# Moving the readout product, two sums and the z projection inside a selective-scan stage

## The chip, the cores and the metric

The kernel runs on one core of one Trainium2 chip. The metric is the device time of that core in microseconds. In the text, PE is TensorE (matmuls), DVE is VectorE, ACT is ScalarE, POOL is GpSimd, and SP is the queue from which most DMAs are issued. Each engine runs its own instructions in order.

## The reference

A convolutional attention layer, then a Mamba block in two directions with a small MLP, then a mixture of two chosen experts. The change lies in the Mamba block alone. Cut to what matters, for each direction:

```
xz = x @ in_proj_w.T                  # 256 -> 1024
xc, z = split(xz)                     # 512 channels each
xc = silu(conv4(xc) + conv_b)         # four taps along the tokens
dt, Bm, Cm = split(xc @ x_proj_w.T)   # 16 + 16 + 16
dt = softplus(dt @ dt_proj_w.T + dt_proj_b)
dA = exp(dt * A);  dBx = dt * Bm * xc # 512 channels x 16 states
h_t = dA_t * h_(t-1) + dBx_t;  y_t = sum over states of h_t * C_t
y = (y + xc * Dp) * silu(z);  out = y @ out_proj_w.T
```

The two directions' outputs are added to m. Then come a layer norm, the MLP `leaky_relu(h @ w1.T + b1) @ w2.T + b2`, the addition of m and of the residual x1, and a second layer norm. There are 4096 tokens, all in float32.

## The kernel before, in words

Four phases follow one another: convolution, attention, Mamba, experts. The Mamba phase (`mamba_phase`, from line 1258) is where everything below happens.

The tokens are cut into 8 chunks of 512. A round is one chunk in one direction, so there are 16 rounds, called i (or q while it is being prepared); even rounds go forward, odd ones backward. A round has 32 slots. A slot n is one (i, e, k, j): one of four channel tiles e, one of four groups of states k, one half j of the tile's channel quarters. Its work is a tile of 128 partitions x 1024. Slot 0 of a round is e = 0, k = 0, j = 0; e changes every 8 slots, k every 2.

The work of a slot:
- `inflow` (POOL, L1894): dbx = dt*x times B, issued two slots ahead, into three buffers.
- `decay` (ACT, L1884): da = exp(dt*A), two instructions into one of two PSUM buffers, one slot ahead.
- `recur` (DVE): the scan over 1024 elements (L1907), and right after it the product with C into one of four h buffers (L1912).
- In slots whose place in the round stands in POOLED, the scan writes h itself, and GpSimd makes the product one slot later (`pooled`, L1917).
- `keep` (ACT, L1938): one slot later, the last state is copied out. The next decay follows it on ACT.
- `bring` (ACT L1932, or POOL L1930 in four slots of a round): adds to dbx what the state brings into the second half of the tile.
- `sum_states` (PE, L1945 and L1947): every second slot, the two h tiles are summed over the states into y, in PSUM, where there is one buffer. A pair whose first slot is pooled is summed one slot later.
- `close` (DVE, L1956): after the last states of a tile, y times z into xc's place. It is in the first slot of the next tile, after that slot's product.

Beside the slots, generators are stepped once per slot:
- `prepare(q)` makes the next round's inputs. It starts at slot 27 of the round before last and goes on through the previous round's slots 0 to 29: projection of x (two PSUM buffers `mm`), four conv sums in slots 3 to 7, SiLU in slot 8, x_proj in slot 9, dt_proj in slots 11 to 15, then softplus. Softplus is max(x,0) + log(1 + exp(-|x|)), with a correction rd that keeps the rounding of 1 + exp: `Identity` of -exp - 1 and then + 1 on ACT (L1425, L1426), three identity matmuls that sum rd, exp and the positive part (L1432, slots 18 to 21), a copy back (L1428), and the logarithm in slot 23 (L1436). GpSimd then adds the logarithm to dt (`dt_piece` with v = 0, L1460) and makes dt*x (v = 1, L1471). Both are written to DRAM, from which `load_dt` reads them back spread over the partitions. The first column of dt goes to DRAM too (`first`, L1465); the carried states are made of it.
- z is projected two tiles at a time in slots 23 and 25 (L1437, L1450) and copied by ACT in slots 24 to 27 (L1448).
- `output(i)` projects the closed round in slots 1 to 3 of the next and adds it to m: by ACT (forward) or DVE (backward, L1536).
- `tail(c)` makes the norms and the MLP of a chunk. It has one PSUM buffer `tl`. Each of its steps names the engine it needs next, and it isn't stepped in slots that FULL lists for that engine. GpSimd adds x1 to m (L1552).

Three functions of ACT need a table load each time they alternate with the decay's exponential: SiLU of z in slot 0 (L2023), SiLU of xc in slot 8 (L1391), and the logarithm in slot 23 (L1436).

The order on each engine is written out by hand. It is the order of these calls, and no scheduler moves anything:

```
inflow(n + 2); keep(n - 1); decay(n + 1); bring(n + 1); recur(n)
load_bc / load_dt; pooled(n - 1); sum_states(n - 3 or n - 2); close
step(out); silu of z; step(prep); step(coming); dt_piece; step(tail)
```

Of the kernel before, what the change touches and what calls it, by code (L numbers as in the profile page):

```python
# [14 lines left out]
FP = mybir.dt.float32  # L15
# [9 lines left out]
P = 128  # L25
# [4 lines left out]
N = 512  # L30
# [1227 lines left out]
def mamba_phase(cx, early, w_in, w_x, w_out, w1, w2, x1d, ud, bcd, dtd, x2d, u2d, usum):  # L1258
# [12 lines left out]
    with ExitStack() as ctx:  # L1271
# [51 lines left out]
        for d in range(2):  # L1323
            for e in range(ET):
                nc.vector.tensor_scalar(
                    skip[d][:, e, :].rearrange("q (j p) -> q j p", j=4), cx.ident.rearrange("q (p j) -> q j p", j=4),
                    cx.col(f"dp{d}", e), None, ALU.mult,
                )
        b1c = one.tile([P, FT], FP, name="b1c")
# [29 lines left out]
        def prepare(q):  # L1359
# [35 lines left out]
            for e in range(ET):  # L1395
                nc.tensor.matmul(ps[0:nx, :], wx[d][:, e, :], xc[:, e, :], start=e == 0, stop=e == ET - 1)
            yield
            xd = few()[0:nx, :]
            nc.scalar.copy(xd, ps[0:nx, :])

# [7 lines left out]
            for e in range(ET + 1):  # L1408
                if e > 0:
                    ex = early.wide("ex")[:, :, 0:N] if e == 1 else ex  # L1410
                    dt = dt or sp.tile([P, ET, N], FP, name="dt", tag="dt")
                    nc.scalar.activation(ex[:, e - 1, :], ps, AF.Abs, bias=cx.col(f"dtb{d}", e - 1))
                    nc.scalar.activation(dt[:, e - 1, :], ps, AF.Relu, bias=cx.col(f"dtb{d}", e - 1))
                if e < ET:
                    ps = mm_psum()
                    nc.tensor.matmul(ps, wdt[r, P * e : P * e + P], xd[r, :], start=True, stop=True)
                yield
# [4 lines left out]
            for e in range(ET + 2):  # L1422
                if e < ET:
                    rd = rds[e] = few()
                    nc.scalar.activation(rd, ex[:, e, :], AF.Identity, scale=-1.0, bias=-1.0)  # L1425
                    nc.scalar.add(rd, rd, 1.0)  # L1426
                if e > 1:
                    nc.scalar.copy(dt[:, e - 2, :], sums.pop(e - 2))  # L1428
                if 0 < e <= ET:
                    ps = sums[e - 1] = mm_psum()  # L1430
                    for v, x in enumerate((rds.pop(e - 1), ex[:, e - 1, :], dt[:, e - 1, :])):
                        nc.tensor.matmul(ps, cx.ident, x, start=v == 0, stop=v == 2)  # L1432
                yield
# [3 lines left out]
            zs = in_pair(q, ET)  # L1437
            yield
            got["dt"] = dt
            for at, (v, e) in enumerate(((0, 0), (1, 0), (0, 1), (0, 2), (0, 3), (1, 1))):  # L1440
                if at == 3 and q > 1:
                    load_first(q, 0)
                dt_piece(q, v, e, ex)
                if at in (0, 2):
                    z = sp.tile([P, 2, N], FP, name="z", tag="z", bufs=3)
                    got.setdefault("z", []).append(z)
                if at < 4:
                    nc.scalar.copy(z[:, at % 2, :], zs[at % 2])  # L1448
                if at == 1:
                    zs = in_pair(q, ET + 2)  # L1450
                    if q + 1 < 2 * NCH:
                        load_u(q + 1)
                yield

        def dt_piece(q, v, e, ex=None, eng=nc.gpsimd):
# [3 lines left out]
            if v == 0:  # L1459
                eng.tensor_tensor(dt[:, e, :], dt[:, e, :], ex[:, e, :], ALU.add)  # L1460
                if q < 2:
                    return
                if e == 0:
                    firsts[q] = ip.tile([P, ET], FP, name="first", tag="first", bufs=1)
                nc.gpsimd.tensor_tensor(firsts[q][:, e : e + 1], dt[:, e, 0:1], odd[:, 0:1], ALU.add)  # L1465
                if e % 2:
                    first_rows[q, e // 2] = cx.rows.tile([P, 2], FP, name="first_row", tag="first_row", bufs=2)
                    nc.sync.dma_start(out=first_rows[q, e // 2], in_=firsts[q][:, e - 1 : e + 1])
# [70 lines left out]
        def tail(c):  # L1539
# [3 lines left out]
            yield from layer_norm(cx, tl, tl_psum, m, hn, nc.gpsimd, 2)  # L1543
            x1 = tl.tile([P, CT, N], FP, name="x1", tag="ln_xc")
            nc.sync.dma_start(out=x1, in_=x1d[c])
            for t in range(CT):
# [3 lines left out]
            yield "DMA"  # L1550
            yield "POOL"
            nc.gpsimd.tensor_tensor(m, x1, m, ALU.add)  # L1552
# [320 lines left out]
        firsts, first_rows, got_first, brought = {}, {}, {}, {}  # L1873
# [26 lines left out]
        def recur(n):  # L1900
# [9 lines left out]
            )  # L1910
            if n % SPS not in POOLED:
                nc.vector.tensor_tensor(h, da, bcs[i, k][1][:, None, :].to_broadcast([P, 2, N]), ALU.mult)  # L1912
# [41 lines left out]
        def close(i, e):  # L1954
# [7 lines left out]
        POOLED = {4, 10, 12, 18, 28}  # L1962
# [7 lines left out]
            "PE": {0, 1, 2, 3, 4, 5, 6, 7, 9, 18, 19, 20, 21, 23, 24, 25, 27, 29},  # L1970
            "ACT": {0, 6, 7, 8, 9, 16, 17, 18, 19, 20, 21, 22, 23, 30, 31},
            "POOL": {0, 1, 2, 4, 24, 25, 26, 27, 28, 29, 30, 31},
# [4 lines left out]
        with tc.manual_schedule(engines=ORDERED):  # L1977
# [5 lines left out]
            for n, (i, e, k, j) in enumerate(slots):  # L1983
# [24 lines left out]
                if j == 0 and n > 0:  # L2008
                    if (n - 2) % SPS not in POOLED:
                        sum_states(n - 2)  # L2010
                    if k == 0:
                        close(*slots[n - 2][:2])
                        if e == 0:
                            out = output(i - 1)
# [24 lines left out]
                if tails and (i == 2 * NCH - 1 or at not in FULL[needs[0]]):  # L2039
                    needs[0] = next(tails[0], None)  # L2040
                    if needs[0] is None:
                        tails.pop(0)
                        needs[0] = "PE"
            ending()
# [307 lines left out]
```

## Time and profile before

| what | us |
|---|---|
| median of 3 runs | 4116.2 (4112.8 to 4122.62) |
| the profiled execution | 4114.68 |
| its span, first to last instruction | 4112.9 |
| first and last scan start | 1940.2 and 3801.4 |
| DVE busy in the span | 3499.8 (85%) |
| PE busy in the span | 3584.9 (87%) |
| ACT busy in the span | 2666.2 (65%) |
| POOL busy in the span | 1839.2 (45%) |

The scans run over 1861 us, with 512 slots in them. The shares over the whole span mix phases with different limits, so the busy times of the scan stage alone count here. In a group's line the numbers are: how many instructions, their busy time together, the mean nanoseconds of one, the engine's idle time just before them, and what ended it. A float32 matmul appears as two records in PE's groups. In a timeline a row is start, duration, engine, line, operation, output and inputs, form, count, and in brackets the idle time before it with what ended that.

### The profile page before, as it was taken

To read this page: it belongs to the slowest core of one execution; us is meant where nothing else is said; L and a number is where in the kernel's file an instruction comes from. 1 tells how busy PE (TensorE), PEld (TensorE's weight loads), DVE (VectorE), ACT (ScalarE), POOL (GpSimd) and SP (SyncE) were. 2 spreads that over 40 slices of the span, in tenths; PEclk is the share of its full clock that TensorE was granted. 3 is DMA by queue.
4 is the path that set the end of the run, shared out by engine and by line. 5 is a ranking of instruction groups with operands and counts; after the bars stand their busy time and mean duration, and the time that the engine had idled before them with its cause. 6 is when DMAs were issued, how large, how long until landed. Compare 5 with 4: busy or idle time off the path is not lost. (4 is left out here: it accounts for less than half of the span.)

```text
span 4112.9 us, 43197 instructions
## 1 busy us (share of the span) xinstructions
PE 3584.9 (87%) x14772; PEld 1175.0 (29%) x14772; DVE 3499.8 (85%) x2908; ACT 2666.2 (65%) x4146; POOL 1839.2 (45%) x1283
## 2 busy tenths in 40 slices
PE   6769888999999999997888888888888888876898
PEld 2324332222222222222222222222222222222343
DVE  8998877989888888877899999999999999999211
ACT  1111226988887888875777778778787778775222
POOL 3020000000000000002888889888888989987000
PEclk9889998999999999998888988998989899988899
DMA  6222215223322322214333344343433334432221
GB/s 208 93 98 96 81 58 157 52 60 65 66 62 55 65 63 57 58 39 138 116 103 121 114 137 139 101 141 106 135 106 127 121 124 120 132 118 80 75 68 35
DMA packets 164051, 399.92 MB, mean 97 GB/s; under 512 B 36981, under 2 KB 45941, under 8 KB 163566
## 3 DMA queue, kind: packets, MB, share of 16 engines
q1 hardware_dynamic: 139198, 312.65, 24.0%
q0 software_dynamic: 24624, 84.43, 8.8%
q8 instruction: 118, 1.93, 0.2%
q14 instruction: 111, 0.91, 0.1%
HBM read 268.16 MB, written 79.56 MB: 85 GB/s over the span
## 5 line engine op out<-in xcount | busy, mean ns | idle before, releaser
L1894 POOL TENSOR_TENSOR dbx<-dtxr,b 128x1024 f32<-128x1024 f32 x512 | 1203.7, 2362 | 197.3 <-DMA dtxr<-dtd 91.3
L1046 ACT ACTIVATE e<-sc 128x1024 f32<-128x1024 f32 x1024 | 993.7, 1023 | 172.0 <-PE sc L1039 147.1
L1907 DVE TENSOR_TENSOR_SCAN da<-da,state,dbx 128x1024 f32<-128x1024 f32 x432 | 1013.9, 2347 | 14.6 <-ACT da L1884 7.2
L956 DVE TENSOR_TENSOR s<-s,e 128x1024 f32<-128x1024 f32 x768 | 880.4, 1216 | 25.0 <-ACT e L1046 24.3
L1884 ACT ACTIVATE da<-dtr,aneg 128x512 f32<-128x512 f32 x1024 | 708.0, 691 | 32.6 <-DMA dtr<-dtd 3.1
L1039 PE MATMUL sc<-q,kS 32*128 32x512 f32 x4096 | 651.9, 648 | 18.6 <-ACT e L1046 13.9
L1912 DVE TENSOR_TENSOR h<-da,c 128x1024 f32<-128x1024 f32 x432 | 529.1, 1225 | 33.1 <-PE y L1947 1.3
L963 PE MATMUL av<-e,vT 128*32 128x512 f32 x4096 | 553.6, 611 | 0.0
L979 POOL DMA_DIRECT2D s<-s x94 | 81.6, 879 | 946.5 <-DVE s L956 856.1
L1947 PE MATMUL y<-h,sel 128*32 128x512 f32 x2048 | 376.1, 664 | 91.6 <-DVE h L1912 66.4
L464 PE MATMUL cv<-v,u 128*128 128x512 f32 x928 | 414.6, 607 | 28.8 <-DVE v L288 13.3
L1039 PEld LDWEIGHTS sc<-q,kS 32*128 32x128 f32 x4096 | 211.4, 185 | 460.7 <-issue 253.1
L1341 PE MATMUL mm<-u,win 128*128 128x512 f32 x464 | 253.6, 697 | 77.6 <-ACT z L1448 25.8
L464 PEld LDWEIGHTS cv<-v,u 128*128 128x128 f32 x928 | 179.4, 195 | 261.7 <-issue 227.8
L562 DVE SCALAR_TENSOR_TENSOR acc<-pad,wdw_s,acc 128x768 f32<-128x768 f32 (+1 forms) x192 | 236.0, 1234 | 19.9 <-ACT acc L555 14.2
L1938 ACT COPY state<-da 128x2 f32<-128x2 f32 x431 | 67.9, 158 | 265.6 <-DVE h L1912 264.7
L143 POOL TENSOR_TENSOR ln_few<-ln_few,minus_half 128x4 f32<-128x4 f32 x29 | 37.4, 1291 | 400.5 <-DMA ln_few<-ln_row 265.4
L1387 PE MATMUL mm<-xp,taps 128*128 128x512 f32 x480 | 213.0, 596 | 0.1
L956 DVE TENSOR_TENSOR s<-e 128x1024 f32<-128x1024 f32 x128 | 151.9, 1217 | 59.5 <-ACT e L1046 59.3
L1907 DVE TENSOR_TENSOR_SCAN h<-da,state,dbx 128x1024 f32<-128x1024 f32 x80 | 187.5, 2344 | 10.6 <-ACT state L1938 9.9
L963 PEld LDWEIGHTS av<-e,vT 128*32 128x32 f32 x4096 | 81.4, 108 | 397.0 <-issue 389.2
L1917 POOL TENSOR_TENSOR h<-h,c 128x1024 f32<-128x1024 f32 x80 | 188.6, 2357 | 1.0 <-ACT state L1938 1.0
(382 smaller groups left out, 3922.1 us busy)
## 6 DMA issues: line engine op xcount, KB each, us to landing
dtr<-dtd SPq DMA_DIRECT2D x128, 512.0 KB
dtxr<-dtd SPq DMA_DIRECT2D x128, 512.0 KB
s<-s POOLq DMA_DIRECT2D x94, 512.0 KB, 6.0
b<-bcd SPq DMA_DIRECT2D x64, 256.0 KB
c<-bcd SPq DMA_DIRECT2D x64, 256.0 KB
dtd<-dt SPq DMA_DIRECT2D x64, 256.0 KB
dtd<-few SPq DMA_DIRECT2D x64, 256.0 KB
u<-uv SPq DMA_DIRECT2D x24, 640.0 KB
```

Source lines behind the costliest of these rows:

```text
L464: nc.tensor.matmul(rows4(ps), u[:, dy, P * ci : P * ci + P], v[:, dy : dy + HR, ci, :], start=dy + ci == 0, stop=dy == k - 1 and ci == CT - 1,
L562: nc.vector.scalar_tensor_tensor(o, src, w_ap, o, ALU.mult, ALU.add)
L956: nc.vector.tensor_tensor(z, x, y, ALU.add)
L963: nc.tensor.matmul(g.av[32 * h : 32 * h + 32, :], vT[:, kb, P * t + 32 * h : P * t + 32 * h + 32], es[h // 2][:, h % 2, :], start=kb == 0, ...
L1039: nc.tensor.matmul(ps[h // 2][:, h % 2, :], kS[r, t, P * kb : P * kb + P], q_t[r, t, :], start=True, stop=True,)
L1046: nc.scalar.activation(e, ps[i], AF.Exp)
L1341: nc.tensor.matmul(ps, win[d][:, t, P * e : P * e + P], u[:, t, ::-1] if d else u[:, t, :], start=t == 0, stop=t == CT - 1,)
L1884: nc.scalar.activation(da[:, v, :], dts[i, e, j][0][:, v, :], AF.Exp, scale=aneg[i % 2][:, a : a + 1])
L1894: nc.gpsimd.tensor_tensor(u, dts[i, e, j][1], bcs[i, k][0][:, None, :].to_broadcast([P, 2, N]), ALU.mult)
L1907: nc.vector.tensor_tensor_scan(das[n].rearrange("p v n -> p (v n)"), da.rearrange("p v n -> p (v n)"), u.rearrange("p v n -> p (v n)"), st ...
L1912: nc.vector.tensor_tensor(h, da, bcs[i, k][1][:, None, :].to_broadcast([P, 2, N]), ALU.mult)
L1947: nc.tensor.matmul(ys[i, e][32 * j : 32 * j + 32, :], cx.sel, hs[n + j // 2][:, j % 2, :], start=False, stop=k == SQ - 1,)
```

## The change

- The product with C leaves `recur` for a function `readout`, called at the end of the slot's calls, after the steps of all generators. `close` and the start of `output` move from slot k = 0, j = 0 to the slot after it (j = 2).
- POOLED goes from five places per round, {4, 10, 12, 18, 28}, to seven, {0, 4, 8, 12, 16, 20, 26}.
- The correction's "+ 1" is no longer an ACT instruction but a matmul of one row of ones by one row of ones into the same sum.
- The logarithm is added to dt by TensorE: two identity matmuls per tile (`dt_sum`), then a copy by ACT and a small copy of the first column (`dt_keep`).
- z's four tiles are projected one at a time in slots 9, 10, 23 and 24 and copied in slots 10, 11, 24 and 25.
- In the tail, x1 is loaded before the norm and added to m by identity matmuls and ACT copies while the norm waits for its DMAs.
- The slots that FULL closes to PE and POOL steps of the tail are other ones.

Cut to its core:

```diff
@@ prepare
             for e in range(ET):
                 nc.tensor.matmul(ps[0:nx, :], wx[d][:, e, :], xc[:, e, :], start=e == 0, stop=e == ET - 1)
+            z_of(q, 0)
             yield
             xd = few()[0:nx, :]
             nc.scalar.copy(xd, ps[0:nx, :])
+            keep_z(q, 0)
+            z_of(q, 1)
...
             for e in range(ET + 1):
+                if e == 0:
+                    keep_z(q, 1)
...
                     nc.scalar.activation(rd, ex[:, e, :], AF.Identity, scale=-1.0, bias=-1.0)
-                    nc.scalar.add(rd, rd, 1.0)
...
                     ps = sums[e - 1] = mm_psum()
-                    for v, x in enumerate((rds.pop(e - 1), ex[:, e - 1, :], dt[:, e - 1, :])):
-                        nc.tensor.matmul(ps, cx.ident, x, start=v == 0, stop=v == 2)
+                    nc.tensor.matmul(ps, cx.ident, rds.pop(e - 1), start=True, stop=False)
+                    nc.tensor.matmul(ps, one1.to_broadcast([1, P]), one1.to_broadcast([1, N]), start=False, stop=False)
+                    nc.tensor.matmul(ps, cx.ident, ex[:, e - 1, :], start=False, stop=False)
+                    nc.tensor.matmul(ps, cx.ident, dt[:, e - 1, :], start=False, stop=True)
...
             nc.scalar.activation(ex, ex, AF.Ln, bias=1.0)
-            zs = in_pair(q, ET)
+            z_of(q, 2)
             yield
             got["dt"] = dt
-            for at, (v, e) in enumerate(((0, 0), (1, 0), (0, 1), (0, 2), (0, 3), (1, 1))):
...
+            keep_z(q, 2)
+            ps = dt_sum(dt, ex, 0)
+            z_of(q, 3)
+            if q + 1 < 2 * NCH:
+                load_u(q + 1)
+            dt_keep(q, 0, ps)
+            yield
+            dt_piece(q, 1, 0)
+            keep_z(q, 3)
+            ps = [dt_sum(dt, ex, e) for e in (1, 2)]
+            yield
+            for e in (1, 2):
+                dt_keep(q, e, ps[e - 1])
+            ps = dt_sum(dt, ex, 3)
+            yield
+            if q > 1:
+                load_first(q, 0)
+            dt_keep(q, 3, ps)
+            yield
+            yield
+            dt_piece(q, 1, 1)
+            yield
+        def z_of(q, e):
+            zs[e] = in_proj(q % 2, gots[q]["u"], ET + e)
+        def keep_z(q, e):
...
+            nc.scalar.copy(gots[q]["z"][e // 2][:, e % 2, :], zs.pop(e))
+        def dt_sum(dt, ex, e):
+            ps = mm_psum()
+            nc.tensor.matmul(ps, cx.ident, dt[:, e, :], start=True, stop=False)
+            nc.tensor.matmul(ps, cx.ident, ex[:, e, :], start=False, stop=True)
+            return ps
+        def dt_keep(q, e, ps):
+            nc.scalar.copy(gots[q]["dt"][:, e, :], ps)
...
+            nc.scalar.copy(firsts[q, h][:, e % 2 : e % 2 + 1], ps[:, 0:1])
@@ tail
-            yield from layer_norm(cx, tl, tl_psum, m, hn, nc.gpsimd, 2)
-            x1 = tl.tile([P, CT, N], FP, name="x1", tag="ln_xc")
+            x1 = tl.tile([P, CT, N], FP, name="x1", tag="a1b")
             nc.sync.dma_start(out=x1, in_=x1d[c])
+            waits = 0
+            for need in layer_norm(cx, tl, tl_psum, m, hn, nc.gpsimd, 2):
...
+                if waits > 1:
+                    nc.scalar.copy(m[:, waits - 2, :], ps)
+                if waits < 3:
+                    ps = tl_psum()
+                    nc.tensor.matmul(ps, cx.ident, m[:, waits - 1, :], start=True, stop=False)
+                    nc.tensor.matmul(ps, cx.ident, x1[:, waits - 1, :], start=False, stop=True)
...
-            yield "DMA"
-            yield "POOL"
-            nc.gpsimd.tensor_tensor(m, x1, m, ALU.add)
@@ the slots
+        def readout(n):
+            i, e, k, j = slots[n]
             if n % SPS not in POOLED:
-                nc.vector.tensor_tensor(h, da, bcs[i, k][1][:, None, :].to_broadcast([P, 2, N]), ALU.mult)
+                nc.vector.tensor_tensor(hs[n], das[n], bcs[i, k][1][:, None, :].to_broadcast([P, 2, N]), ALU.mult)
...
-        POOLED = {4, 10, 12, 18, 28}
+        POOLED = {0, 4, 8, 12, 16, 20, 26}
...
-            "PE": {0, 1, 2, 3, 4, 5, 6, 7, 9, 18, 19, 20, 21, 23, 24, 25, 27, 29},
+            "PE": {0, 1, 2, 3, 4, 5, 6, 7, 9, 10, 18, 19, 20, 21, 24, 25, 26, 27, 29},
...
-            "POOL": {0, 1, 2, 4, 24, 25, 26, 27, 28, 29, 30, 31},
+            "POOL": {1, 2, 4, 5, 9, 11, 13, 17, 21, 25, 27, 29, 30, 31},
...
-                    if k == 0:
-                        close(*slots[n - 2][:2])
-                        if e == 0:
-                            out = output(i - 1)
+                if j == 2 and k == 0 and n > 2:
+                    close(*slots[n - 3][:2])
+                    if e == 0:
+                        out = output(i - 1)
...
+                readout(n)
```

## The prediction

> **What bounds the kernel now.** I read the page first, then the busy times of the scan stage by stretches, VectorE's waits there, and the timelines of VectorE and ScalarE, slot by slot.
>
> ```profile
> span 4112.9 us, 43197 instructions
> ...
> L1894 POOL TENSOR_TENSOR dbx<-dtxr,b 128x1024 f32<-128x1024 f32 x512 | 1203.7, 2362 | 197.3 <-DMA dtxr<-dtd 91.3
> ...
> L1907 DVE TENSOR_TENSOR_SCAN da<-da,state,dbx 128x1024 f32<-128x1024 f32 x432 | 1013.9, 2347 | 14.6 <-ACT da L1884 7.2
> ...
> L1912 DVE TENSOR_TENSOR h<-da,c 128x1024 f32<-128x1024 f32 x432 | 529.1, 1225 | 33.1 <-PE y L1947 1.3
> ```
>
> The reader sees the two VectorE instructions of a slot and how little VectorE idles before them. The next answer gives busy times over 1625 us inside the scan stage (the sum of four stretches from 2060 to 3685): VectorE 96%, GpSimd 88%, TensorE 84%, ScalarE 78%.
>
> ```profile
> sum 1625.00, PE 1372.08 PEld 447.03 DVE 1567.23 ACT 1270.51 POOL 1430.53; mean PE 343.02 PEld 111.76 DVE 391.81 ACT 317.63 POOL 357.63
> ```
>
> So VectorE sets the pace, and only its time, or a wait of its own, moves the end. VectorE's timeline prices a slot: a pooled slot (line 1) takes 2.26 from scan to scan, a plain one (lines 2 to 4) 3.50, up to 3.60 elsewhere.
>
> ```profile
> 2883.24 2.34 DVE L1907 TENSOR_TENSOR_SCAN h<-da,state,dbx 128x1024 f32<-128x1024 f32 x1
> 2885.50 2.33 DVE L1907 TENSOR_TENSOR_SCAN da<-da,state,dbx 128x1024 f32<-128x1024 f32 x1
> 2887.86 1.23 DVE L1912 TENSOR_TENSOR h<-da,c 128x1024 f32<-128x1024 f32 x1
> 2889.00 2.35 DVE L1907 TENSOR_TENSOR_SCAN da<-da,state,dbx 128x1024 f32<-128x1024 f32 x1
> ```
>
> The second limit is ScalarE where it switches tables. Slot 8 of a round starts at 2896.18; ScalarE's timeline:
>
> ```profile
> 2896.30 0.16 ACT L1938 COPY state<-da 128x2 f32<-128x2 f32 x1 [0.82 <-DVE h L1912]
> 2896.49 1.42 ACT L1884 ACTIVATE da<-dtr,aneg 128x512 f32<-128x512 f32 x2
> 2897.93 1.28 ACT L1391 ACT_TABLE_LOAD   x1
> 2899.22 1.91 ACT L1391 ACTIVATE xc<-xc 128x2048 f32<-128x2048 f32 x1
> 2901.04 0.14 ACT L1938 COPY state<-da 128x2 f32<-128x2 f32 x1
> 2901.20 1.28 ACT L1884 ACT_TABLE_LOAD   x1
> 2902.49 1.42 ACT L1884 ACTIVATE da<-dtr,aneg 128x512 f32<-128x512 f32 x2
> 2903.84 0.28 ACT L1932 ACTIVATE dbx<-dbx,brought 128x1 f32<-128x1 f32 x1
> ```
>
> The decay that slot 10 needs, and the added carry behind it, end 7.9 us after slot 8 began. The chain can't start sooner: its first copy waits for the product of slot 7. So two slots can't take less than 8.0 here, whatever VectorE saves in them. The same chain stands at slot 0 (SiLU of z: 8.05) and at slot 23 (logarithm).
>
> **The change, part by part.** A round is 32 slots, one i; 16 rounds. All in us.
>
> *Two more products per round to GpSimd.* A plain slot averages 3.56, a pooled one 2.26: 1.30 each, 2.6 per round, 41.6 in all. The Trainium skill (Perfetto Trace Analysis, "Optimizing Scalar/DVE Operations") speaks against it: GpSimd and VectorE share an SBUF read port, so moving work between them might not help. By it the 41.6 could be 0. By the trace the product takes 1223/1225/1226 ns (min/median/max of 432) beside a GpSimd that is 88% busy, and a pooled slot is 1.30 shorter. I take the row. GpSimd pays 2 x 2.36 = 4.7 per round and loses four adds (1.18 each), four small ones (0.19) and half an x1 add (2.36/2): 6.7. It gets no fuller; its inputs run up to two slots ahead, and the worst burst (slots 0 to 5) is about 3 us beyond VectorE's pace, inside that lead: cost 0; uncovered it would be those 3 per round.
>
> *The product behind the slot's other work.* After a scan, an independent instruction starts 2.26 after the scan's start; a dependent product 2.38 to 2.46. With a close, an m add or a tail step between, that gap of about 0.15 goes: some 8 times per round, 1.1. Closing a slot later also drops waits of the kind "close waits for y", 13.0 us in VectorE's waits.
>
> So VectorE's own work falls from about 114.1 to 110.2 per round. What it waits for is now the question.
>
> *TensorE.* Added per round: four rank-1 matmuls, eight for dt plus logarithm, and four per two rounds for x1: 14 x 0.89 (L1387: 213.0 us for 240 matmuls) = 12.4, so 84% becomes about 95%. No row shows a 1-row matmul; the 16-row one (L1416) streams the same 512 columns and is no shorter, so 0.89, bounds 0.4 and 1.4 (83.1 us for 60 of L1416, with its waits). Moving z costs nothing.
>
> *ScalarE.* Lost: four adds (0.63). Gained: four copies (0.57), four small ones (0.16 to 0.19), one copy of m. Equal within 0.8 per round, but the copies stand at slots 24 to 27, behind the logarithm, and each waits for TensorE; decay, and so the next scan, is queued behind them. The x1 load goes ahead of the norm's DMAs on SP; its buffer has been free for tens of slots: 0. The rows for the carry leave within a few us of before: 0.
>
> *New waits of VectorE.* Pooled slots now stand four apart, and there are four h buffers: the scans of 4, 8, 12, 16, 20 wait for the y sums of the slot just before, and all of VectorE stands behind. By adding up TensorE's queue at 0.89 each, those sums end 0 to 2 us ahead of need, except about 0.4 late at slot 16 in every other round.
>
> Stretch by stretch, before (mean of rounds 2 to 14, by starts of the scans) and after:
> - 0 to 2: 8.26, after 8.07. Slot 0 pooled would give 2.26 + 4.00 = 6.26, but the table chain holds it: 1.8 lost.
> - 2 to 8: 20.65, after 21.08 (5 x 3.56 + 2.26; two m adds at 0.45 and the 1.13 reduction, which now falls here, in every other round).
> - 8 to 10: 8.21, after 8.00. Again the table chain, not 6.26.
> - 10 to 16: 20.84, after 21.05 (one pooled slot fewer here).
> - 16 to 18: 8.53, after 6.55. Slot 16 has an exponential but no table load; ScalarE is done at 5.7.
> - 18 to 22: 12.96, after 13.42 (a tail step).
> - 22 to 26: 15.51, after 16.7. Four matmuls per piece end the fourth sum near 4.2 after slot 22, so its copy ends at 4.8; decay of 24, load, logarithm, load, decay of 25 and carry take 7.9 more: scan 25 at 12.8 against 10.7 by VectorE. The close that gave cover there has moved behind scan 25. Then 4.0.
> - 26 to 32: 21.60, after 20.85.
>
> Sum 116.56 to 115.72: -0.84 per round. Of 3.9 less work about 3.0 comes back as waits. On the table loads the skill (ScalarE: Activation LUTs, "What ACT_TABLE_LOAD costs") adds about 1.38 of drain to the load of 1.28. In the trace the load starts 0.02 after its predecessor's end and is followed 0.01 after its own, so each chain is 7.9; by the page it would be 10.6, and stretch 8 to 10 could not have been 8.21. I use the row.
>
> 14 rounds x -0.84 = -11.8; first round -2 (its close waited 2.55 for y), last -2 (no preparation), the ending -1 (the last tail is no longer drained in it). I add 4.6 (a third of a microsecond per round) for collisions that I did not resolve. Sum -12. The profiled execution took 4114.7 (span 4112.9), 1.5 below the median 4116.2; on the median: 4104.
>
> **Rivals.**
> 1. ScalarE's chain does not hold (state copies wait for the scan alone, decays come earlier): the lost 3.0 and most of before's 2.4 fall away. 3.9 x 16 = 62: 4054. For it: the copy after a pooled scan starts 0.03 after its end. Against: every plain copy starts with the product's end. 12%.
> 2. Slower: TensorE late in slots 3 to 22. If its queue runs 1 us later than I add up (a rank-1 matmul at 1.4, a cold clock: the granted clock is 0.89 here), scans of 8, 12, 16 wait about 0.8 each and scan 25 one more: 3.4 per round, 2.6 net, x 15 = +38: 4150; a half of that gives 4130. It decides from 0.25 us late per event, where 0.84 is eaten. For it: TensorE at 95%, in order. Against: sums of dt came at the same place within 1 us in all rounds. 22%.
> 3. The change does not do what it says for the time: the logarithm's stretch takes all of it, 0.7 longer per round than I have: 4115. 28%.
>
> My own case, 4085 to 4107, has 38%.
>
> **Numbers.** A measurement of this kernel tells about 0.2% (8 us) from no change. Faster than 4108: 38 + 12 = 0.50; within: 0.28; slower: 0.22. The range 4072 to 4138 leaves out most of rival 1 and the far half of rival 2.
>
> **What would show it.** Right: scans of slots 2 and 10 wait 1 to 2 us for ScalarE's decay or carry in every round, scan 25 about 2 us; the product rows 400 and 112; VectorE about 94% busy; the stretch 16 to 18 near 6.5. Wrong: pooled scans that wait for y by more than 0.5 us; 22 to 26 over 18; or stretches 0 to 2 and 8 to 10 under 7.

## The result, and the profile after

The changed kernel takes 4182.4 us (median of 4 runs, 4173.6 to 4185.3), the kernel before 4117.8 (4 runs): ratio 1.0144, with a 95% interval of 1.0126 to 1.0161. (The two medians alone give 1.0157, inside that interval.) It is slower by 1.4%. The prediction said 4104, with a range of 4072 to 4138.

The profiled execution took 4181.2. First the lines of its page that answer to those of before: the span, then the groups of the inputs on GpSimd, the plain scans and their products.

```profile
span 4179.4 us, 44052 instructions
...
L1938 POOL TENSOR_TENSOR dbx<-dtxr,b 128x1024 f32<-128x1024 f32 x512 | 1205.1, 2361 | 244.4 <-DMA dtxr<-dtd 109.5
...
L1951 DVE TENSOR_TENSOR_SCAN da<-da,state,dbx 128x1024 f32<-128x1024 f32 x400 | 939.2, 2348 | 118.6 <-ACT dbx L1981 59.5
...
L1961 DVE TENSOR_TENSOR h<-da,c 128x1024 f32<-128x1024 f32 x400 | 488.4, 1221 | 23.9 <-DVE da L1951 0.5
```

The durations are those of before. What is new is the idle time ahead of the plain scans: 118.6 us in place of 14.6, half of it behind the carry that ScalarE adds to dbx (L1981). The busy times over the same 1625 us of the scan stage say it again: VectorE falls from 1567 to 1487 (92%), TensorE rises from 1372 to 1447 (89%).

```profile
sum 1625.00, PE 1446.65 PEld 483.06 DVE 1487.27 ACT 1241.44 POOL 1372.33; mean PE 361.66 PEld 120.77 DVE 371.82 ACT 310.36 POOL 343.08
```

From the first scan's start to the last one's the stage takes 1918.0 against 1861.1: +56.9 of the 66.5 us by which the spans differ. (Over all kernels below the first scan started between 1925 and 1947; what makes the difference ahead of it is not known. So stretches inside the stage are compared, with the medians beside them.) The first round has +11.0, the second +6.2, rounds 2 to 14 together +45.3, the last round -5.5. By stretch of a round, as in the prediction (mean of rounds 2 to 14, even and odd ones weighted alike):

| slots | before | forecast | after |
|---|---|---|---|
| 0 to 2 | 8.26 | 8.07 | 8.16 |
| 2 to 8 | 20.65 | 21.08 | 21.38 |
| 8 to 10 | 8.21 | 8.00 | 8.03 |
| 10 to 16 | 20.84 | 21.05 | 21.40 |
| 16 to 18 | 8.53 | 6.55 | 6.55 |
| 18 to 22 | 12.96 | 13.42 | 14.23 |
| 22 to 26 | 15.51 | 16.7 | 18.63 |
| 26 to 32 | 21.60 | 20.85 | 21.51 |
| round | 116.54 | 115.72 | 119.89 |

Three stretches came as forecast within 0.1 (0 to 2, 8 to 10, 16 to 18), two within 0.35 (2 to 8, 10 to 16). The one at the logarithm, 22 to 26, took 1.9 more than forecast, its neighbours 0.8 and 0.7 more.

TensorE's timeline of one such place (round 8; slot 18 starts at 2980.70, slot 22 at 2994.71). A piece is one channel tile's sum of softplus. The first and the fourth one, with what follows each:

```profile
2979.16 1.42 PE L1436 MATMUL mm<-few,ident 128*128 128x512 f32 x2 [3.93 <-ACT few L1431]
2980.51 2.07 PE L1437 MATMUL mm<-ident 1*128 1x512 f32 x2
2982.51 2.08 PE L1438 MATMUL mm<-ex,ident 128*128 128x512 f32 x2
2984.38 1.91 PE L1439 MATMUL mm<-dt,ident 128*128 128x512 f32 x2
2986.08 1.32 PE L1994 MATMUL y<-xc,skip 128*128 128x512 f32 x2
2987.34 1.06 PE L1996 MATMUL y<-h,sel 128*32 128x512 f32 x8
...
2997.28 1.02 PE L1436 MATMUL mm<-few,ident 128*128 128x512 f32 x2
2998.23 1.12 PE L1437 MATMUL mm<-ident 1*128 1x512 f32 x2
2999.28 1.13 PE L1438 MATMUL mm<-ex,ident 128*128 128x512 f32 x2
3000.25 1.02 PE L1439 MATMUL mm<-dt,ident 128*128 128x512 f32 x2
3001.20 1.06 PE L1996 MATMUL y<-h,sel 128*32 128x512 f32 x8
```

Read the starts: the fourth piece takes 3001.20 - 2997.28 = 3.92, not 3.56. The one-row matmul (L1437) stands 1.05 from its successor, and the full matmuls beside it stand 0.95 and 0.97 from theirs, where three in a row stand 0.86 apart. The first piece follows 3.93 of idle time and takes 6.92, with 1.4 to 2.0 for a matmul; the granted clock over it was 0.55, over the fourth piece 1.00. The fourth sum is there 6.6 after slot 22 began. ScalarE's timeline from there:

```profile
2997.48 0.59 ACT L1433 COPY dt<-mm 128x512 f32<-128x512 f32 x1 [2.81 <-PE mm L1439]
...
3001.30 0.59 ACT L1433 COPY dt<-mm 128x512 f32<-128x512 f32 x1 [1.51 <-PE mm L1439]
...
3003.42 1.28 ACT L1443 ACT_TABLE_LOAD   x1
3004.72 1.91 ACT L1443 ACTIVATE ex<-ex 128x2048 f32<-128x2048 f32 x1
...
3009.34 0.28 ACT L1981 ACTIVATE dbx<-dbx,brought 128x1 f32<-128x1 f32 x1
```

The copy waits for the sum, the chain of the two table loads follows it, and the carry that scan 25 needs ends 14.9 after slot 22 began. VectorE's scans of slots 20 and 25, the first behind the y sum that follows the cold piece:

```profile
2988.51 2.35 DVE L1951 TENSOR_TENSOR_SCAN h<-da,state,dbx 128x1024 f32<-128x1024 f32 x1 [0.67 <-PE y L1996]
...
3009.65 2.36 DVE L1951 TENSOR_TENSOR_SCAN da<-da,state,dbx 128x1024 f32<-128x1024 f32 x1 [2.46 <-ACT dbx L1981]
```

In the waits of the scan stage (total, times, longest) the two sides stand out, VectorE's on ScalarE and ScalarE's on the sums; in the kernel before, these copies' wait for their sums is not among the seven rows that ScalarE's list shows (5.8 us and up).

```profile
DVE da L1951 <- ACT dbx L1981: 59.5, 42, 2.5
...
DVE h L1951 <- PE y L1996: 17.7, 17, 1.9
```

```profile
ACT dt L1433 <- PE mm L1439: 87.7, 45, 3.5
ACT dt L1487 <- PE mm L1481: 36.1, 30, 1.8
```

### The profile page after: what moved, and what is told of

Its sections match the earlier page's. It is cut to its first block, busy times and chain, and to the rows that moved or that the text cites. A ratio compares the mean times of both kernels' runs of the same rounds, so it can differ in the third digit from the quotient of the medians.

```text
span 4179.4 us, 44052 instructions
## 1 busy us (share of the span) xinstructions
PE 3717.8 (89%) x15188; PEld 1228.0 (29%) x15188; DVE 3455.7 (83%) x2876; ACT 2673.6 (64%) x4216; POOL 1819.9 (44%) x1192
## 5 line engine op out<-in xcount | busy, mean ns | idle before, releaser
L1938 POOL TENSOR_TENSOR dbx<-dtxr,b 128x1024 f32<-128x1024 f32 x512 | 1205.1, 2361 | 244.4 <-DMA dtxr<-dtd 109.5
L1951 DVE TENSOR_TENSOR_SCAN da<-da,state,dbx 128x1024 f32<-128x1024 f32 x400 | 939.2, 2348 | 118.6 <-ACT dbx L1981 59.5
L1961 DVE TENSOR_TENSOR h<-da,c 128x1024 f32<-128x1024 f32 x400 | 488.4, 1221 | 23.9 <-DVE da L1951 0.5
L1996 PE MATMUL y<-h,sel 128*32 128x512 f32 x2048 | 316.3, 620 | 52.4 <-DVE h L1961 41.9
L1951 DVE TENSOR_TENSOR_SCAN h<-da,state,dbx 128x1024 f32<-128x1024 f32 x112 | 262.3, 2342 | 27.3 <-PE y L1996 17.7
L1342 PE MATMUL mm<-u,win 128*128 128x512 f32 x464 | 238.7, 654 | 38.9 <-ACT z L1476 32.5
L1966 POOL TENSOR_TENSOR h<-h,c 128x1024 f32<-128x1024 f32 x112 | 264.0, 2357 | 6.5 <-ACT state L1987 6.3
```

Of the source, the lines that this page charges most:

```text
L1342: nc.tensor.matmul(ps, win[d][:, t, P * e : P * e + P], u[:, t, ::-1] if d else u[:, t, :], start=t == 0, stop=t == CT - 1,)
L1938: nc.gpsimd.tensor_tensor(u, dts[i, e, j][1], bcs[i, k][0][:, None, :].to_broadcast([P, 2, N]), ALU.mult)
L1951: nc.vector.tensor_tensor_scan(das[n].rearrange("p v n -> p (v n)"), da.rearrange("p v n -> p (v n)"), u.rearrange("p v n -> p (v n)"), st ...
L1961: nc.vector.tensor_tensor(hs[n], das[n], bcs[i, k][1][:, None, :].to_broadcast([P, 2, N]), ALU.mult)
L1966: nc.gpsimd.tensor_tensor(hs[n], hs[n], bcs[i, k][1][:, None, :].to_broadcast([P, 2, N]), ALU.mult)
L1996: nc.tensor.matmul(ys[i, e][32 * j : 32 * j + 32, :], cx.sel, hs[n + j // 2][:, j % 2, :], start=False, stop=k == SQ - 1,)
```

## The experiments

Two theories went into the runs. S: the sums of softplus end late on TensorE, ScalarE's copies wait for them, and with them the logarithm and the scans of slots 22 to 29. P: the seven pooled places cost the time. The table shows each kernel's ratio to the kernel before in runs on the same chip, then its profiled stage (first to last scan start), and mean stretches of rounds 2 to 14.

| kernel | median | ratio, interval | stage | 10-16 | 18-22 | 22-26 | 26-32 | round |
|---|---|---|---|---|---|---|---|---|
| before | 4117.8 | | 1861.1 | 20.84 | 12.96 | 15.51 | 21.60 | 116.54 |
| after | 4182.4 | 1.0144 [1.0126, 1.0161] | 1918.0 | 21.40 | 14.23 | 18.63 | 21.51 | 119.89 |
| e1 | 4126.6 | 1.0029 [1.0016, 1.0043] | 1873.1 | 21.55 | 13.44 | 15.59 | 21.56 | 117.36 |
| e2 | 4110.9 | 0.9986 [0.9975, 0.9997] | 1860.0 | 20.03 | 12.96 | 15.60 | 21.65 | 116.49 |
| e3 | 4204.5 | 1.0212 [1.0183, 1.0242] | 1950.9 | 22.80 | 13.52 | 17.29 | 23.00 | 121.94 |
| e4 | 4138.7 | 1.0062 [1.0041, 1.0083] | 1894.1 | 21.60 | 13.31 | 15.51 | 21.93 | 118.20 |
| e5 | 4093.4 | 0.9942 [0.9925, 0.9958] | 1846.5 | 21.48 | 13.45 | 15.58 | 20.45 | 114.84 |
| e6 | 4129.9 | 1.0048 [1.0029, 1.0066] | 1895.8 | 21.34 | 13.57 | 17.91 | 21.52 | 118.44 |
| e7 | 4179.8 | 1.0158 [1.0141, 1.0175] | 1919.1 | 21.30 | 14.33 | 18.56 | 20.94 | 119.45 |
| e8 | 4137.5 | 1.0055 [1.0038, 1.0072] | 1886.3 | 22.37 | 12.96 | 15.51 | 21.67 | 118.16 |
| e9 | 4114.3 | 0.9998 [0.9984, 1.0012] | 1871.4 | 19.53 | 13.60 | 15.56 | 21.10 | 116.99 |
| e10 | 4095.3 | 0.9955 [0.9937, 0.9973] | 1839.9 | 20.10 | 13.32 | 15.60 | 21.51 | 115.00 |
| e11 | 4101.4 | 0.9973 [0.9957, 0.9989] | 1849.5 | 20.20 | 13.69 | 15.60 | 21.53 | 115.61 |
| e12 | 4128.3 | 1.0050 [1.0030, 1.0071] | 1875.2 | 20.99 | 13.42 | 17.13 | 21.60 | 117.04 |
| e13 | 4241.1 | 1.0322 [1.0297, 1.0347] | 1988.2 | 21.18 | 16.53 | 20.92 | 21.29 | 124.26 |
| e14 | 4113.4 | 1.0004 [0.9992, 1.0015] | 1859.7 | 20.00 | 13.40 | 15.56 | 22.10 | 116.05 |
| e15 | 4141.2 | 1.0074 [1.0055, 1.0093] | 1887.9 | 21.31 | 13.67 | 15.63 | 22.80 | 117.93 |

### The parts alone: e1 to e4

e1 is the changed kernel with the whole `prepare` of before (log by GpSimd, + 1 by ScalarE, z in pairs):

```diff
-                    nc.tensor.matmul(ps, one1.to_broadcast([1, P]), one1.to_broadcast([1, N]), start=False, stop=False)
+                    nc.scalar.add(rd, rd, 1.0)
...
-            ps = dt_sum(dt, ex, 0)
-            z_of(q, 3)
...
+            zs = in_pair(q, ET)
...
+                dt_piece(q, v, e, ex)
```

> The changed kernel with the preparation of the kernel before (z in pairs, + 1 on ScalarE, logarithm added by GpSimd); readout, seven pooled slots, tail and FULL as changed. Theory S (the sums of softplus on TensorE come late and hold ScalarE, which holds the scans of slots 22 to 29): the loss goes, 4090 to 4120, and the stretch from slot 22 to 26 falls from 18.6 to under 16.5. Theory P (the pooled slots, four apart, and their y sums cost it): 4160 to 4185, as the whole change.

Stretch 22 to 26 falls to 15.59, as S said, and 4182 falls to 4126.6. But that is above the 4120 expected at most and still slower than before (1.0029), so the rest of the change brings no gain.

e2 is the kernel before with `readout` and the later `close` alone:

```diff
-                nc.vector.tensor_tensor(h, da, bcs[i, k][1][:, None, :].to_broadcast([P, 2, N]), ALU.mult)
...
+                readout(n)
...
-                    if k == 0:
-                        close(*slots[n - 2][:2])
+                if j == 2 and k == 0 and n > 2:
+                    close(*slots[n - 3][:2])
```

> The kernel before with only the product behind the slot's other work and the close one slot later. Both theories: some eight gaps of 0.15 per round and most of the 13 us in which the close waits for y, so 15 to 30 us less: 4088 to 4103. If the late close takes cover from slot 25, it is 10 us less of a gain. Slower than 4118 would be against both.

A small gain, 0.14%, well short of the 15 to 30 us expected. It saves 0.8 in slots 10 to 16 and 1.0 in 16 to 18, and gives 0.7 and 0.6 back in 2 to 8 and 8 to 10.

e3 is the kernel before with the new `prepare` alone, e4 the kernel before with the seven places alone:

```diff
-        POOLED = {4, 10, 12, 18, 28}
+        POOLED = {0, 4, 8, 12, 16, 20, 26}
```

> The kernel before with only the new preparation (z in other slots, + 1 by a one-row matmul, logarithm added by TensorE). Theory S: 2 to 3.5 us per round more and about 8 in the first round: 4150 to 4175, with ScalarE's copies of dt waiting for TensorE. Theory P: 4110 to 4125.

> The kernel before with only the other places of pooled slots: seven instead of five. Theory S: the 2.6 us per round are eaten by the table loads at slots 0 and 8 or nearly: 4095 to 4122. Theory P: 4140 to 4170, with pooled scans that wait for y.

The new preparation alone costs more than the whole change, and 30 us more than S had at most; the seven places cost about 25 us, which lies between the ranges of the two theories. Of e4's +33 in the stage, 21 lie in rounds 2 to 14 and 8.5 in the last round. So P is the smaller part and the preparation the larger one; how much of that is S, the next runs tell.

### The parts of the preparation: e5 to e8

e5 undoes one line of the change: the + 1 is ScalarE's again.

```diff
                     nc.scalar.activation(rd, ex[:, e, :], AF.Identity, scale=-1.0, bias=-1.0)
+                    nc.scalar.add(rd, rd, 1.0)
...
-                    nc.tensor.matmul(ps, one1.to_broadcast([1, P]), one1.to_broadcast([1, N]), start=False, stop=False)
```

> The changed kernel with one thing undone: the + 1 of the correction is an instruction of ScalarE again, and a piece of softplus is three matmuls instead of four. Theory S (the sums of softplus end late on TensorE, hold ScalarE's copies, and so the logarithm and the scans of slots 22 to 29): the one-row matmul measured 1.05 us in a warm piece and about 2.0 in the cold first one, so the fourth sum ends 1.05 x 3 + 2.0 = 5.1 earlier as far as TensorE sets it, and the copies then wait for the slots instead. Stretch 22 to 26 falls from 18.63 to about 16.3, 18 to 22 by 0.5; 15 rounds x 2.8 = 42: 4140 (4125 to 4155). Theory P (it is the seven pooled places that cost): nothing there changes, 4175 or more.

4093.4: faster than both kernels, and 32 below the lowest that S had given. The change's loss hangs on this one line: 18 to 32 falls by 4.9 per round. Of the copies that waited 87.7 us in 45 places for their sums, 5.3 in 10 are left.

```profile
2942.29 1.02 PE L1437 MATMUL mm<-few,ident 128*128 128x512 f32 x2
2943.15 1.02 PE L1438 MATMUL mm<-ex,ident 128*128 128x512 f32 x2
2944.01 1.02 PE L1439 MATMUL mm<-dt,ident 128*128 128x512 f32 x2
2944.96 1.06 PE L1996 MATMUL y<-h,sel 128*32 128x512 f32 x8
```

```profile
ACT dt L1434 <- PE mm L1439: 5.3, 10, 1.8
```

The fourth piece takes 2.67 here (starts 2942.29 to 2944.96). One one-row matmul had made it 3.92: it costs 1.25, not 0.89.

e6 keeps four matmuls and lets the one-row one go first, while TensorE waits for rd:

```diff
-                    nc.tensor.matmul(ps, cx.ident, rds.pop(e - 1), start=True, stop=False)
-                    nc.tensor.matmul(ps, one1.to_broadcast([1, P]), one1.to_broadcast([1, N]), start=False, stop=False)
+                    nc.tensor.matmul(ps, one1.to_broadcast([1, P]), one1.to_broadcast([1, N]), start=True, stop=False)
+                    nc.tensor.matmul(ps, cx.ident, rds.pop(e - 1), start=False, stop=False)
```

> The changed kernel with the order of two matmuls changed: the one-row matmul opens each piece's sum instead of following the matmul of rd, so TensorE can do it while it waits for ScalarE's rd. The number of matmuls is unchanged. Theory S with a cold clock (the first piece costs 6.9 because TensorE idles 3.93 ahead of it): the first piece after rd has three matmuls and a shorter idle time ahead of it, so it ends some 2 to 3 us sooner and the whole row of pieces with it: 22 to 26 from 18.63 to about 16.9, 4155 (4140 to 4168). If the four matmuls per piece alone set it, at 4.0 per piece whatever comes before: only the first one's 1.05 is saved, 4170 or more. Theory P: no change.

The median, 4129.9, lies below the range given; the runs scatter from 4123.6 to 4149.1, and the profiled one is among the slower (4142.7; its stage is 22 shorter than after's). In even rounds, where TensorE idles ahead of the first piece, 22 to 26 falls from 18.93 to 17.46; in odd rounds, where it doesn't, the mean stays (18.34 and 18.37). So the order matters most at the first piece after an idle time, and the later pieces (3.82 each, 3.92 to 4.02 in the changed kernel) keep most of the rest.

e7 lets GpSimd add the logarithm again (`dt_piece` with v = 0 in place of `dt_sum` and `dt_keep`); z stays in its new slots.

```diff
-            ps = dt_sum(dt, ex, 0)
...
-            dt_keep(q, 0, ps)
...
+            for at, (v, e) in enumerate(((0, 0), (1, 0), (0, 1), (0, 2), (0, 3), (1, 1))):
...
+                dt_piece(q, v, e, ex)
```

> The changed kernel with GpSimd adding the logarithm to dt again, as before the change; z stays in its new slots and the pieces keep four matmuls. Theory S says that the pieces (slots 18 to 22) are what is late, and the eight matmuls for dt come after the logarithm: stretch 22 to 26 stays at 18 or more, 26 to 32 falls by up to 0.9 (21.5 to 20.6), GpSimd has 5.5 more to do per round: 4172 (4160 to 4185). The rival within the preparation, that it is the matmuls and copies of dt in slots 24 to 29 that hold ScalarE: 22 to 26 falls to about 16.5 and the time to 4130 to 4150.

As S said: 22 to 26 stays (18.56), 26 to 32 falls by 0.6. The matmuls for dt are cleared of the loss at the logarithm. The whole time is the same (4179.8), because the first two rounds grew by 6.6.

e8 is the kernel before with z's projections alone in slots 9, 10, 23 and 24.

```diff
+            z_of(q, 0)
             yield
             nc.scalar.copy(xd, ps[0:nx, :])
+            keep_z(q, 0)
+            z_of(q, 1)
```

> The kernel before with z's four projections alone moved to slots 9, 10, 23 and 24. The prediction said that moving z costs nothing: 4110 to 4120. The rival: in the kernel before with the whole new preparation the stretch 10 to 16 grew by 2.0, with copies of z that wait 32 us in all for TensorE in slots 10 and 11; if the z moves are the reason, 10 to 16 grows by 1 to 2 here too and the time is 4130 to 4145.

The rival was right: 10 to 16 grows by 1.5. ScalarE's timeline in slots 11 and 12 of round 8, and VectorE's scan of slot 12:

```profile
2915.51 0.58 ACT L1400 COPY few<-mm 48x512 f32<-48x512 f32 x1 [3.67 <-PE mm L1396]
2917.42 0.58 ACT L1463 COPY z<-mm 128x512 f32<-128x512 f32 x1 [1.34 <-PE mm L1341]
...
2919.45 0.28 ACT L1942 ACTIVATE dbx<-dbx,brought 128x1 f32<-128x1 f32 x1
```

```profile
2919.77 2.35 DVE L1917 TENSOR_TENSOR_SCAN h<-da,state,dbx 128x1024 f32<-128x1024 f32 x1 [3.37 <-ACT dbx L1942]
```

The scan waits for the carry, not for z's matmul. What costs is the copy: it waits 1.34 on ScalarE for that matmul, and the decay and the carry of slot 12 are queued behind it. In the kernel before, that decay starts 0.68 after the `few` copy (2910.05 and 2910.73 in round 8), here 2.59 after it. The scans of slot 12 waited 27.5 us in all, 8.5 in the kernel before.

### Form or number: e12 and e13

e12 keeps four matmuls per piece but adds the 1 with 128 rows; e13 adds a second one-row matmul, of zeros.

```diff
-                    nc.tensor.matmul(ps, one1.to_broadcast([1, P]), one1.to_broadcast([1, N]), start=False, stop=False)
+                    nc.tensor.matmul(ps, cx.ident, ones1.to_broadcast([P, N]), start=False, stop=False)
```

> The changed kernel with the one-row matmul replaced by one of 128 rows that adds the same 1: the identity by a column of ones read 512 times. The number of matmuls is that of the change, only its form differs. If it is a fourth matmul that costs (theory S by count): a piece of all-128-row matmuls takes 4 x 0.87 = 3.5 (the three-matmul pieces with + 1 on ScalarE took 2.6) instead of 3.9, the fourth copy comes about 1.5 earlier, 22 to 26 falls from 18.6 to about 17.3: 4163 (4150 to 4175). If the one-row form is what costs (theory F: switching between 1 and 128 rows makes it and its neighbours slow): the time falls to 4130 to 4145. If neither form matters: 4175 to 4190.

```diff
+                    nc.tensor.matmul(ps, one1.to_broadcast([1, P]), zero1.to_broadcast([1, N]), start=False, stop=False)
```

> The changed kernel with a second one-row matmul in each piece, which adds a row of zeros, so that nothing but the dose of the suspected cost changes. Theory S: one such matmul took a piece from 2.6 to 3.9, so each piece gets 1.0 to 1.3 longer again and the fourth copy comes 4 to 5 later; 22 to 26 and 18 to 22 together grow by 4 to 5 per round as nothing is left to cover it: 4245 (4225 to 4265). If TensorE is not what holds these slots: below 4200.

e13 came as expected: 4241.1, and 18 to 26 together grew by 4.6 per round. The sum was made otherwise than forecast: a piece at full speed grew by 0.86 (4.78 against 3.92), not by 1.0 to 1.3, and a cold first one by about 2 (8.0 to 9.3 against 6.6 to 7.6). e12's time, 4128.3, is just below the range of theory F, and its 22 to 26 (17.13) is where the count put it (17.3): both hold a share. Its first piece after 4.55 of idle time, and its fourth:

```profile
2931.37 2.08 PE L1437 MATMUL mm<-few,ident 128*128 128x512 f32 x2 [4.55 <-ACT few L1432]
2933.24 1.63 PE L1438 MATMUL mm<-ones,ident 128*128 128x512 f32 x2
2934.70 1.02 PE L1439 MATMUL mm<-ex,ident 128*128 128x512 f32 x2
2935.56 1.02 PE L1440 MATMUL mm<-dt,ident 128*128 128x512 f32 x2
2936.42 1.02 PE L1995 MATMUL y<-xc,skip 128*128 128x512 f32 x2
...
2946.54 1.02 PE L1437 MATMUL mm<-few,ident 128*128 128x512 f32 x2
...
2950.06 1.06 PE L1997 MATMUL y<-h,sel 128*32 128x512 f32 x8
```

The fourth piece takes 3.52, between 2.67 and 3.92: of the 1.25, 0.85 is the fourth matmul and 0.40 its form. The first piece takes 5.05 against 6.92: here full speed is back from its third matmul on, there not before the piece's end. Per round, from after to e12 to e5: 119.89, 117.04, 114.84. The form has 2.85 of the 5.05, the number 2.2 (with what ScalarE's + 1 costs in e5). The ratios put it the other way round, 0.9% and 1.1% (e12's profile is the fastest of its five executions), so it is about half each.

### Versions: e9 to e11, e14 and e15

e9 is the changed kernel with the preparation and the five places of before. e10 and e11 are e2 with other places.

```diff
-        POOLED = {0, 4, 8, 12, 16, 20, 26}
+        POOLED = {4, 10, 12, 18, 28}
```

> The changed kernel with the preparation of before and the five pooled places of before: what is left of the change is the product behind the slot's work, the later close, x1 added by TensorE and the tail's other slots. Against the readout alone (0.9986 of before) it tells what the tail's part is worth. Theory S has nothing to say here and expects the same, 4105 to 4117; if the places of the tail's steps cost, 4122 to 4135 and the seven pooled places are cleared of what the changed kernel with the preparation of before showed (1.0029).

```diff
-        POOLED = {4, 10, 12, 18, 28}
+        POOLED = {4, 10, 12, 16, 20, 28}
```

> The kernel before with the product behind the slot's other work, and six pooled places, 4, 10, 12, 16, 20, 28: none where a table load of ScalarE sets the stretch (slots 0, 8, 22 to 25), and 16, which gave its full gain in the changed kernel (16 to 18 took 6.55). Against the readout alone: 16 to 18 from 7.57 to about 6.5, place 20 instead of 18 leaves 18 to 22 as it is. Round 116.5 to 115.4, 15 x 1.1 = 16: 4095 (4088 to 4103). If pooled places cost whatever their slot (theory P): 4110 to 4125.

```diff
-        POOLED = {4, 10, 12, 18, 28}
+        POOLED = {4, 10, 12, 16, 18, 20, 28}
```

> As the six places, and 18 pooled as well: 4, 10, 12, 16, 18, 20, 28. If VectorE's own work sets the stretch 18 to 22, it falls from 12.96 to about 11.7 and the time to 4078 (4070 to 4090). If GpSimd can't keep up with three products in six slots beside its inputs (each 2.36, inputs 2.36 per slot, so 21 us of work in 16.5), the gain is lost in scans that wait for dbx in slots 20 to 24: 4095 to 4110.

The tail's part is worth nothing that can be told (0.9998, and the interval of e2 overlaps; the profile is of the slowest of e9's ten executions). Against e1 (1.0029) only the places differ: in the changed kernel without its preparation the seven cost 0.3%. Six places away from the table loads gain as expected (4095.3), though in part by luck: of the 1.5 per round only 0.6 came at 16 to 18, 1.2 came in 2 to 10, where none was forecast, and 18 to 22 gave 0.4 back. A seventh gains no more: e11 lies in the second range given for it, but not for the reason given. No scan waited for dbx from GpSimd in slots 20 to 24; the scan of slot 20 waited 26.0 us in 14 places for y (6.2 in 8 in e10), which is the wait of theory P.

e14 is e5 with those six places; e15 is e10 with the new preparation, + 1 on ScalarE.

> The changed kernel with + 1 on ScalarE (0.9942 of before) and six pooled places, 4, 10, 12, 16, 20, 28, in place of the seven. Against that run: 0 to 2 and 8 to 10 stay at about 8.1 to 8.5, 10 to 16 falls from 21.5 to about 20.2, the first round from 128 to about 124: 4073 (4063 to 4085) if the places at table loads are worth nothing; if GpSimd's and TensorE's relief was what made that run fast and the places don't matter, 4088 to 4098.

> The kernel before with the product behind the slot's work, six pooled places (0.9955 of before) and the new preparation with + 1 on ScalarE; the tail is that of before. The logarithm on TensorE takes 5.5 per round from GpSimd and shortened 26 to 32 by 1.1 in the changed kernel with + 1 on ScalarE. Round 115.0 to 113.9: 4077 (4065 to 4090). If z's projections in slots 9 and 10 delay the pooled places 10 and 12 as they did in the kernel before (10 to 16 longer by 1.5): 4095 to 4105.

Both missed. In e14, 10 to 16 fell by 1.5 as expected, but 8 to 10 rose from 8.13 to 8.98 and 26 to 32 from 20.45 to 22.10. With place 28 in place of 26 the scan of slot 29 waited 22.1 us in 13 places for ScalarE's carry, in e5 never. In e15, 10 to 16 is 1.2 longer than in e10, as the rival for z had it (the scans of slot 12 waited 13.5 us in place of 3.1), and 26 to 32 is 1.3 longer: in slots 27 and 29 VectorE waited 8.8 us for the tail's sum on TensorE and 8.4 us for ScalarE's decay and carry, in e10 for neither. The gains do not add up. The fastest are e5 and e10, and their intervals overlap.

## Why the prediction was wrong

**The step that failed:** "Four matmuls per piece end the fourth sum near 4.2 after slot 22, so its copy ends at 4.8". The sum ended 6.6 after slot 22 in round 8 (6.5 counted to the next matmul's start, as below; 0.2 in the kernel before), its copy at 7.2. The mechanism was named and the place was right; the term was mis-sized. With four full matmuls the sum holds: in e12's odd rounds 5 to 13, where nothing is cold, the fourth sum ends 4.0 after slot 22, scan 25 comes at 12.5 and 22 to 26 takes 16.5 (forecast 4.2, 12.8, 16.7). What it missed:

- The one-row matmul was put at 0.89. It took 1.25 with its effect on its neighbours (3.92 against 2.67 for the piece), inside the prediction's own bounds of 0.4 and 1.4: 4 x 0.36 = 1.4 more per round. In rounds 5, 7, 9 and 13 of the changed kernel, where nothing is cold, the fourth sum ends 5.6 after slot 22, just that 1.4 late.
- In even rounds the first piece ran at about half speed after an idle time: 6.92 against 3.92, 3.0 more. A cold clock stood in rival 2 as a cause, but no sum had it. Where it bites, slot 22 is itself held back: only 0.9 of it shows after slot 22 (the fourth sum at 6.5). More shows ahead of it. The y sum for scan 20 stands behind the cold piece on TensorE, scan 20 waited 8.8 us in 8 places for it, and 18 to 22 took 14.34 in even rounds against 12.88 in e12's. Rounds 3 and 11, where the first piece was not cold but began 1.7 later, came to 6.5 as well.
- The copies of the earlier pieces wait too (87.7 us in 45 places with the fourth), and scan 23 waited 14.7 us in 13 places behind them. The prediction let only the fourth one wait. Scan 25, which ends the chain, is set by the fourth.

The next step held. From the copy's end (3001.89) to the carry's (3009.62) is 7.7; forecast 7.9. So scan 25 came at 14.9 after slot 22 instead of 12.8 (12.7 by the prediction's own terms): 2.1 in this round, and the stretch's 1.9 in the mean. The close that had given cover there before stood behind scan 25, as the prediction said, so nothing absorbed it.

**"22 to 26 over 18"** was the sign named for being wrong, and it is what the trace shows (18.63). Another sign of being wrong came too, pooled scans that wait for y by more than 0.5: 17.7 us in 17 places, nearly all in slots 16 (7.9) and 20 (8.8). These waits fall in the stretches 10 to 16 and 18 to 22, which came 0.35 and 0.8 late.

**VectorE's own work.** Right: 400 and 112 scans, a pooled slot 2.26, VectorE 92% busy for 94% forecast, 16 to 18 at 6.55.

**TensorE at 95%.** It was 89% busy. So the busy share was overstated while the queue in one stretch was understated; the share did not show the lateness.

**The table chains.** Right for the changed kernel: slots 0 and 8 gave next to nothing against before (8.16 for 8.26, 8.03 for 8.21), and the scans of slots 2 and 10 waited for ScalarE 1.6 and 1.1 us each, though in 12 and 7 places and not in every round. But with the product behind the slot's work and a plain slot 8, the stretch takes 8.30 (e10) to 8.98 (e14): there the place pays for the product's new position.

**GpSimd at cost 0.** Nearly: in the stage VectorE waited 10.2 us for GpSimd's carry (L1979; 2.4 before), 0.6 more per round, in slots 1 and 9, whose stretches came as forecast. It has no row of a wait for GpSimd's inputs (L1938), and GpSimd fell from 88% to 84%.

**"Moving z costs nothing."** Wrong. Alone it cost 0.55% (e8), by the wait of its copy on ScalarE. In the changed kernel 10 to 16 missed its forecast by 0.35 only.

**Slots 26 to 32**, forecast 20.85, measured 21.51. Copies of dt waited 36.1 us for their sums, and scan 29 waited 11.5 us for ScalarE; with the pieces on time (e5) it was 16.9 and nothing, and the stretch 20.45. The forecast was about right without the delay that reached it.

**The first rounds.** Forecast -2 for the first, measured +11.0 and +6.2 for the first two. Alone, the new preparation costs 10.5 in the first round and the seven places 4.1. The prediction took it for a small matter and never costed it; what in it costs is not settled (e5 keeps 8.2 of the 11.0).

**The rivals.** Rival 2 had the right causes (a one-row matmul that costs more than 0.89, a cold clock), given 22%. Of its places, scan 25 waited in rounds 1 to 14 (34.7 us in 14 places, where the kernel before has no such row), scan 16 in six; scans 8 and 12 hardly waited, and scan 20, which it did not name, did. Its price, 4150, was 32 too low. Rival 3, the logarithm's stretch 0.7 longer, was 1.9. Rival 1 did not occur: the state copies still wait for the product (197.2 us in 192 places).

## What to carry to other kernels

An engine with idle time on average can still be late in one stretch: add up its queue there with the durations of that stretch, the cold ones and those of a new form too, and ask whose in-order queue waits for the end. A copy out of PSUM is a wait on the copying engine, and what is queued behind it pays. When a change loses, undo its smallest line first: here one instruction per piece decided between 1.4% slower and 0.6% faster.

## What the runs showed of the hardware

At full speed a one-row float32 matmul of 512 columns was in no run shorter than a full one. Between full ones it is longer: 1.05 against 0.86 from start to start, and the full matmuls beside it take 0.95 to 0.97 (after, round 8). Two of them in a row (e13) take 0.97 and 0.95, and the second lengthens the piece by 0.86, as a fourth full one does by 0.85 (e12). What sets the 1.05 stays open.

It also seems not to bring the clock back. In the even rounds from 2 to 14 the first piece follows 3.6 to 4.6 us of idle time. With full matmuls alone (e12) it reached full speed 3.3 us (round 8) to 5.2 us (round 2) after its start; in round 8 the granted clock was 0.54 over the first 3.33 us and 1.00 after that. With one one-row matmul in it (after) its last matmul was still slow, 6.6 to 7.6 us after the start, and with two (e13) at 8.0 to 9.3. The Trainium skill (TensorE: Matmul & The Clock Gate, Part 1: The HAM clock gate) says that about 3.4 us of sustained activity restore the clock, whatever the number of matmuls. The runs with full matmuls agree roughly; those with one-row matmuls do not. That the row count is the reason was not tested by itself.
